# A recommendation network on one core: row transfers issued half by SyncE and half by ScalarE

## The chip, the cores and the metric

The kernel runs on one core of a Trainium2 chip. Its time is the device time of that core in microseconds (us), taken over several runs. Beside the times there is one profiled execution, whose trace holds every instruction of the five engines: PE (TensorE, matmuls; PEld are its weight loads), DVE (VectorE), ACT (ScalarE), POOL (GpSimd) and SP (SyncE). SP does no arithmetic; it only issues transfers. ACT and POOL issue transfers beside their own work. PEq, ACTq, SPq and so on are the sequencers, the parts of the engines that wait, load registers and issue transfers.

## The reference

The batch has 16384 samples. Each sample has 32 token numbers, three lists of 20 numbers, and four single numbers. All of them pick rows from tables:

```python
tok = word_emb[token_idx].mean(axis=1)      # 50000 x 300 table, 32 rows a sample
e1 = emb_mh1[mh1_idx].mean(axis=1)          # 1000 x 64, 20 rows a sample; e2: 5000 rows, e3: 10000
o1 = emb_oh1[oh1_idx]                       # 100 x 64; o2, o3, o4 alike
emb = jnp.concatenate([tok, e1, e2, e3, o1, o2, o3, o4], axis=1)     # 748 columns
wide = wide_mh1[mh1_idx].sum(...) + ... + wide_oh4[oh4_idx][:, 0]    # one number a sample
h = relu(emb @ W1 + b1)                     # 748 -> 1024
h = relu(h @ W2 + b2)                       # 1024 -> 512
h = relu(h @ W3 + b3)                       # 512 -> 256
return sigmoid(h @ Wd + bd + wide)          # 256 -> 1
```

All of it is float32. The token rows are the heavy part: 16384 x 32 rows of 1200 bytes.

## The kernel before, in words

The batch is cut into 128 tiles of 128 samples, one sample on each partition. Four kinds of work go on at once, and the kernel's main loop writes their instructions into one order by hand. The loop has 128 x 11 + 27 = 1435 steps, eleven for a tile and some at the end; what a step emits is the order in which each engine works it off.

**Small tables, by counting (PE, DVE, ACT).** The seven small tables stay in SBUF. In each step `one_hots` (line 501, DVE) compares index digits with a ramp and makes one-hot columns `hot`; ACT multiplies the upper half by 256 (line 508); `counts` (line 519, PE) multiplies pairs of one-hots into PSUM tiles `pc`; ACT copies them to `cnt` (line 522). There are two `hot` buffers and two `pc` buffers, and `hot` is made one step before PE uses it. `small_sums` (line 554, PE) multiplies the counts of the last tile with the tables, and DVE reduces the result into the feature tile `g` (line 544).

**The network (PE, ACT).** `g` is transposed by PE (line 595) and scaled by DVE into `x` (line 599); blocks of three tiles go through the three layers (line 677), and ACT applies bias and relu to each part of `h` (line 688). `ph` has two PSUM buffers.

**Token rows, by gather (POOL, DVE).** POOL issues an indirect transfer for each token place of a tile (line 337): it reads one row of the word table for each of the 128 samples into half of a buffer `tok_rows`. Six buffers hold two token places (a group) each. Three groups later (`TOK_LAG`) DVE adds the two halves to the tile's sum (lines 312, 314, 319). A buffer is free for the next gather when DVE has added it.

**Token rows, one by one (SP, ACT).** For some tiles a token place isn't gathered by POOL, and its 128 rows come as 128 single transfers of 1200 bytes whose addresses are registers (`fetch` on SP, `ScalarRows` on ACT):

- The column of 128 token numbers is loaded as one line (`load_column`), DVE turns it into byte offsets (lines 370, 371), and the queue's engine loads them into registers (line 375, TENSOR_LOAD: SP 32 at a time, ACT 8).
- SP fetches the last token place (31) of all tiles from 4 on whose number isn't a multiple of three: 83 tiles. `FETCH_AHEAD` says how many steps before the sum is due the fetch begins, `FETCH_STEPS` over how many steps its rows are spread in the order, `COLUMN_AHEAD` and `COLUMN_LAG` when column and offsets come.
- ACT fetches the last place but one (30) of tiles that `choose` picks: the first tile whose sum is due late enough for 128 rows at `SCALAR_RATE` rows a step and a margin of 5 steps. It does so for 26 tiles. Addresses are loaded at most twice a step, eight when fewer than eight are left (two when rows were issued just before).

What sets the order between these two is the lane. Every transfer of SP and ACT takes the next of eight semaphores (lanes) in a turn, and a lane's next transfer waits until its last one has landed. `transfers` holds the order over both queues. Lanes 6 and 7 of the turn belong to ACT: before SP takes one of them, `sync_dma` asks ScalarE for a row, and SP takes the lane itself only where ScalarE has no address ready:

```python
while len(transfers) % LANES in SCALAR_LANES and scalar_row and scalar_row[0]():
    pass
hardware_dma(nc.sync, **operands)
```

So in a turn of eight SP issues six and ACT two. ACT's rows stand in ACT's own order between the instructions on `hot`, `cnt` and `h`; an ACT row that waits holds up what stands behind it. The code line of all these transfers is line 161. SP also loads the indices of every pair of tiles, the weights at the start, and stores the outputs.

Of the kernel before, what the change touches and what calls it, by code (L numbers as in the profile page):

```python
# [26 lines left out]
TOK_BUFS = 6  # L27
HOT_BUFS = 2
FETCH_FROM = 4
FETCH_STEPS = 16.5  # L30
FETCH_AHEAD = {1: 25.0, 2: 19.5}
COLUMN_AHEAD = 4
COLUMN_LAG = 1
LOADS = 32
LANES = 8
SCALAR_LANES = (6, 7)
SCALAR_FROM = 12
SCALAR_RATE = 2.55
SCALAR_MARGIN = 5.0
SCALAR_LOADS = 8  # L40
SCALAR_WANTED, SCALAR_LEAST = 8, 2
# [43 lines left out]
def kernel(  # L85
# [85 lines left out]
    def sync_dma(**operands):  # L171

        while len(transfers) % LANES in SCALAR_LANES and scalar_row and scalar_row[0]():
            pass
# [222 lines left out]
    class ScalarRows:  # L397
# [9 lines left out]
        def choose(self, rows_before):  # L407

            least = self.step + (rows_before + P) / SCALAR_RATE + SCALAR_MARGIN
            t = next((t for t in range(tiles_all) if self.summed_at(t) >= least), None)  # L410
# [371 lines left out]
    tiles = B // P  # L782
# [13 lines left out]
    def summed_at(t):  # L796

        n = n_groups * (t + 1) + TOK_LAG
        return n / FRONT_PACE if n < front else FRONT_STEPS + (n - front) / pace

    fetches = [(summed_at(t) - FETCH_AHEAD[t % 3], t) for t in range(FETCH_FROM, tiles) if t % 3]
    fetching = []

    columns_due = []
# [1 line left out]
    def fetch_rows(step, part):  # L806
# [19 lines left out]
        for at, rows in list(fetching):  # L826
            rows.to(P * (step + part - at) / FETCH_STEPS)
            if step + part - at >= FETCH_STEPS:
                rows.finish()
# [9 lines left out]
    scalar = ScalarRows(summed_at, column_due)  # L839
    scalar_first = int(summed_at(SCALAR_FROM) - (P / SCALAR_RATE + 15))  # L840

# [29 lines left out]
    for step in range(n_steps):  # L871
        t, i = divmod(step, STEPS)
# [124 lines left out]
```

## Time and profile before

| | |
|---|---|
| time, median of 3 runs | 5021.99 us (5021.95 to 5024.2) |
| the profiled execution's own time | 5021.06 us |
| its span, first to last instruction | 5019.3 us |
| granted TensorE clock, mean | 0.990 |
| gathers on POOL (line 337) | 3987, 3773.3 us busy, 1219.3 us idle before them |
| rows issued by SP / by ACT | 10624 / 3328 |
| ACT busy / idle before its work | 2726.5 us / of which 1664.0 us waiting for DVE's `hot` |
| DMA engines, mean busy share; data | 0.48 in the steady part; 654 MB in all |

A line of a group of instructions names its code line, engine, operation, and what it writes and reads (out<-in), then how many there were, the shortest, median and longest duration in ns. "Idle before" is the time that the engine did nothing before such instructions, with what ended it. A wait line reads: who waited, for whom, us in total, how often, the longest. In a timeline each line is a start, a duration and an instruction; "x101" are so many alike that follow each other. The busy time of a sequencer (SPq, ACTq) isn't counted in the engine's busy share, so ACT's 54% holds none of its transfers.

### The profile page before, as it was taken

The numbers are of one execution on the slowest core, as the hardware profiler recorded it, in microseconds if no ns is written. First come the engines' busy times: TensorE is split into PE (matmuls) and PEld (weight loads), VectorE is DVE, ScalarE is ACT, GpSimd is POOL, SyncE is SP. The second block draws the span as 40 slices with busy tenths as digits, with TensorE's granted clock in tenths as the row PEclk, the third lists the DMA queues.
The fourth block names the chain that finished last, engine by engine and source line by source line (L and its number), as shares of the span: only waits on it lengthen the run. The fifth ranks groups of instructions, "written<-read, shape, count | busy, mean of one in ns | idle before, by whom it ended". The sixth has DMA issues, their size and how long they took to land.

```text
span 5019.3 us, 124363 instructions
## 1 busy us (share of the span) xinstructions
PE 4806.3 (96%) x36356; PEld 3721.3 (74%) x36356; DVE 3748.7 (75%) x6830; ACT 2726.5 (54%) x3658; POOL 3774.2 (75%) x3994
## 2 busy tenths in 40 slices
PE   6799999999999999999999999999999999999999
PEld 4577777777777777777777777667767888888899
DVE  6777777777777777777777777777777777777774
ACT  5455555555555555555555555555555555555552
POOL 7777777777777777777777777777777777777775
PEclk8899999999999999999999999999999999999999
DMA  7444444444444444444444444444444444444443
GB/s 204 127 129 130 129 129 129 129 130 129 129 130 128 129 130 129 130 129 129 129 129 129 130 129 129 130 129 129 130 130 129 129 129 130 130 129 130 129 128 100
DMA packets 291735, 654.13 MB, mean 130 GB/s; under 512 B 147100, under 2 KB 161692, under 8 KB 291048
## 3 DMA queue, kind: packets, MB, share of 16 engines
q0 software_dynamic: 191376, 612.66, 45.1%
q1 hardware_dynamic: 89271, 29.49, 2.7%
q10 hardware_dynamic: 10400, 4.02, 0.4%
q8 instruction: 284, 4.65, 0.4%
q14 instruction: 404, 3.30, 0.2%
HBM read 645.65 MB, written 0.07 MB: 129 GB/s over the span
## 4 chain that ended last, share of the span: by engine, by line
PE 37%; DMA 26%; DVE 15%; issue 12%; POOL 9%; ACT 1%; SPq 1%; ACTq 0%; DVEq 0%; POOLq 0%
DMA tok_rows<-in_word_emb_dram,it 23%; PE ph L677 17%; PE pg L554 14%; POOL tok_rows L337 9%; DVE hot L501 5%; DVE own L319 4%; PE pc L519 4%; DVE own L314 3%; DMA fetched_scalar<-in_word_emb_dram 1%; DMA fetched<-in_word_emb_dram 1%; PE pc L595 1%; DVE g L544 1%; PE po L719 1%; SPq L161 1%; DVE x L599 0%
## 5 line engine op out<-in xcount | busy, mean ns | idle before, releaser
L337 POOL DMA_INDIRECT tok_rows<-in_word_emb_dram,it x3987 | 3773.3, 946 | 1219.3 <-issue 754.1
L508 ACT ACTIVATE hot<-hot 64x768 bf16<-64x768 bf16 (+1 forms) x1408 | 1155.4, 821 | 1820.6 <-DVE hot L501 1664.0
L554 PE MATMUL pg<-terms,cnt 128*128 128x195 bf16 x17664 | 1723.7, 249 | 35.6 <-DVE g L544 35.0
L554 PEld LDWEIGHTS <-cnt 128*128 128x128 fp8e3 x17664 | 1529.2, 98 | 83.1 <-issue 54.4
L677 PE MATMUL ph<-x,w_sb 128*128 128x384 f32 (+5 forms) x4932 | 1473.8, 437 | 16.2 <-ACT h L688 11.9
L501 DVE TENSOR_TENSOR hot<-own,sc 128x1656 bf16<-128x1656 bf16 (+1 forms) x1408 | 1393.7, 990 | 126.7 <-PE pc L519 37.7
L522 ACT ACTIVATE cnt<-pc 128x828 uint16<-128x828 f32 (+1 forms) x1408 | 1186.5, 843 | 181.5 <-PE pc L519 103.2
L319 DVE TENSOR_TENSOR own<-own,tok_rows 128x300 f32<-128x300 f32 x1792 | 857.1, 478 | 513.3 <-DMA tok_rows<-in_word_emb_dram,it 468.5
L677 PE MATMUL ph<-h,w_sb 128*128 128x384 f32 (+2 forms) x4160 | 1225.9, 435 | 14.2 <-ACT h L688 14.0
L314 DVE TENSOR_TENSOR own<-own,tok_rows 128x300 f32<-128x300 f32 x1827 | 873.8, 478 | 271.9 <-DMA tok_rows<-in_word_emb_dram,it 221.0
L677 PEld LDWEIGHTS ph<-x,w_sb 128*128 128x128 f32 (+1 forms) x4932 | 830.8, 191 | 305.7 <-ACT h L688 23.0
L519 PEld LDWEIGHTS <-hot 128*128 128x128 bf16 x8192 | 594.2, 98 | 523.8 <-issue 271.3
L677 PEld LDWEIGHTS ph<-h,w_sb 128*128 128x128 f32 x4160 | 700.6, 191 | 266.1 <-ACT h L688 27.3
L519 PE MATMUL pc<-hot 128*128 128x138 bf16 x8192 | 733.1, 225 | 111.8 <-ACT hot L508 51.7
L688 ACT ACTIVATE h<-ph,b_sb 128x384 f32<-128x384 f32 (+2 forms) x723 | 378.7, 524 | 210.5 <-PE ph L677 115.4
L544 DVE TENSOR_REDUCE g<-pg 128x130 f32<-128x390 f32 (+1 forms) x512 | 259.2, 506 | 140.0 <-PE pg L554 138.7
L599 DVE TENSOR_TENSOR x<-pc,scale 128x768 f32<-128x768 f32 x127 | 120.8, 951 | 58.8 <-PE pc L595 57.5
L595 PE MATMUL pc<-ident,g 128*128 128x128 f32 x762 | 107.3, 278 | 5.7 <-ACT cnt L522 5.4
L312 DVE TENSOR_TENSOR own<-tok_rows 128x300 f32<-128x300 f32 x128 | 61.5, 481 | 55.3 <-DMA tok_rows<-in_word_emb_dram,it 52.6
L595 PEld LDWEIGHTS pc<-ident,g 128*128 128x128 f32 x762 | 83.7, 143 | 9.8 <-ACT cnt L522 9.3
L488 DVE COPY sc<-pc 128x512 bf16<-128x512 bf16 x64 | 44.0, 688 | 40.5 <-PE pc L484 39.8
L719 PE MATMUL po<-h,wd_sb 128*1 128x384 f32 (+2 forms) x208 | 67.4, 442 | 4.4 <-ACT h L688 4.4
(59 smaller groups left out, 514.6 us busy)
## 6 DMA issues: line engine op xcount, KB each, us to landing
fetched<-in_word_emb_dram SPq DMA_DIRECT2D x10624, 1.2 KB
tok_rows<-in_word_emb_dram,it POOLq DMA_INDIRECT x3987
fetched_scalar<-in_word_emb_dram ACTq DMA_DIRECT2D x3328, 1.2 KB
ix<-in_idx_dram SPq DMA_DIRECT2D x64, 64.0 KB
w_sb<-in_W_dram SPq DMA_DIRECT2D x6, 512.0 KB
raw<-in_mh_dram SPq DMA_DIRECT2D x4, 682.5 KB
it<-in_idx_dram SPq DMA_DIRECT2D x64, 32.0 KB
w_sb<-in_W_dram SPq DMA_DIRECT2D x1, 2048.0 KB
```

Source lines behind the costliest of these rows:

```text
L314: nc.vector.tensor_add(tok_sum, tok_sum, a)
L319: nc.vector.tensor_add(to, tok_sum, b)
L337: gather = nc.gpsimd.indirect_dma_start(out=rows[-1], out_offset=None, in_=word, in_offset=bass.IndirectOffsetOnAxis(ap=it[:, j : j + 1], ...
L501: nc.vector.tensor_tensor(hot[:, 0 : 2 * rows, :].rearrange("p i (n d) -> p i n d", d=2), iota.rearrange("p (n d) -> p n d", d=2).unsqueez ...
L508: nc.scalar.activation(upper, upper, AF.Copy, scale=UPPER)
L519: nc.tensor.matmul(pc[:, k // n, at : at + n_h], hot[:, 2 * k, 0:P], hot[:, 2 * k + 1, :], start=True, stop=True)
L522: nc.scalar.activation(cnt[:, :, b : b + rows].rearrange("l h (g k) -> l h g k", g=2), pc[:, :, 0 : n * n_h].rearrange("l g (k h) -> l h g ...
L544: nc.vector.tensor_reduce(field_columns(features(t), pair), pg[:, 0:n, :].rearrange("p f (c d) -> p f d c", c=3), AX.X, ALU.add,)
L554: nc.tensor.matmul(pg[:, j, :], by_slice[:, h, :], terms[:, h, :], start=(h == h0), stop=(h == h1 - 1))
L595: nc.tensor.transpose(pt[:, j // n, j % n, :], g[:, c : c + P], ident)
L677: nc.tensor.matmul(to, weights[: src.shape[0], k, m * P : (m + 1) * P], src, start=(k == 0), stop=(k == len(srcs) - 1),)
L688: nc.scalar.activation(dst()[:, m, 0:n], ph[:, 0:n], AF.Relu, bias=bias[:, m : m + 1])
```

## The change

The turn of lanes is dealt out anew: lanes 2, 3, 6 and 7 belong to ScalarE, so that a turn is two of SP, two of ACT, two of SP, two of ACT. SP fetches the last token place of every second tile (the odd ones from 5 on, 62 tiles for 83), each spread over 22 steps and begun 25.5 steps ahead. ACT's rate, by which `choose` picks the next tile, goes from 2.55 to 5.6 rows a step; ACT then fetches the last place but one of 53 tiles for 26. POOL's gathers go from 3987 to 3981. The order of all compute instructions on PE, DVE and ACT is the same in both kernels.

```diff
-FETCH_STEPS = 16.5
-FETCH_AHEAD = {1: 25.0, 2: 19.5}
+FETCH_STEPS = 22.0
+FETCH_EVERY = 2
+FETCH_AHEAD = {1: 25.5}
...
-SCALAR_LANES = (6, 7)
+SCALAR_LANES = (2, 3, 6, 7)
 SCALAR_FROM = 12
-SCALAR_RATE = 2.55
+SCALAR_RATE = 5.6
...
-    fetches = [(summed_at(t) - FETCH_AHEAD[t % 3], t) for t in range(FETCH_FROM, tiles) if t % 3]
+    fetches = [
+        (summed_at(t) - FETCH_AHEAD[t % FETCH_EVERY], t)
+        for t in range(FETCH_FROM, tiles)
+        if t % FETCH_EVERY in FETCH_AHEAD
+    ]
```

## The prediction

> **What bounds the kernel now.** I read the page's busy shares first. PE is at 96% and POOL at 75%, so PE looks like the bound; the second view, the instructions of the gather line L337, corrects that.
>
> ```profile
> PE 4806.3 (96%) x36356; PEld 3721.3 (74%) x36356; DVE 3748.7 (75%) x6830; ACT 2726.5 (54%) x3658; POOL 3774.2 (75%) x3994
> ```
> ```profile
> L337 POOL DMA_INDIRECT tok_rows<-in_word_emb_dram,it x3987: 942/946/1233, 2.8 to 4993.1; - x200
> ...
>   issue: 754.1, 2473
> ```
>
> A gather takes 946 ns, and the idle time before it is 754.1/2473 = 0.305 us, nearly always the same. Busy and idle time of the line are 3773.3 + 1219.3 = 4992.6 us over 3987 gathers, 1.252 us each, from 2.8 us to the end of the last at 4994.0. POOL therefore issues without a break for the whole run; only 18 of its starts lie over 1.3 us apart, and all that they lose is 5.4 us. After the last gather come 25.3 us of tail. POOL sets the time. But PE has little room, as the windows show (columns: busy us of PE, PEld, DVE, ACT, POOL, then clock and DMA share):
>
> ```profile
> 0.00:125.00 125.00, 84.16 (x496) 52.80 (x496) 78.35 (x157) 74.68 (x112) 93.49 (x105) 0.89 0.75 204
> 250.00:4900.00 4650.00, 4519.97 (x34082) 3487.59 (x34081) 3530.19 (x6404) 2560.97 (x3395) 3516.72 (x3717) 1.00 0.48 129
> ```
>
> Between 250 and 4900 us PE is idle for 130 us of 4650 (2.8%), at full clock. So there are two near-bounds, and whatever delays PE by more than that shows in the time. PE's waits in that stretch:
>
> ```profile
> PE pc L519 <- DVE x L599: 40.4, 39, 2.5
> PE pg L554 <- DVE g L544: 25.8, 30, 2.2
> PE ph L677 <- ACT h L688: 24.8, 29, 3.3
> PE pc L519 <- DVE sc L488: 11.9, 11, 2.0
> PE pc L519 <- ACT hot L508: 9.3, 14, 2.5
> ```
>
> Only waits of the counts (L519) on work that stands on DVE between gather-paced additions can shrink when gathers get fewer: 40.4 + 11.9 + 9.3 = 62 us. The rest are hand-overs.
>
> The third view is the two queues that issue single rows. Both also load addresses into registers (TENSOR_LOAD; 8 rows each on ACT, 32 on SP):
>
> ```profile
> L161 ACTq DMA_DIRECT2D fetched_scalar<-in_word_emb_dram x3328: 213/214/746, 309.9 to 4790.8; - x196
> L375 ACTq TENSOR_LOAD <-columns x416: 716/763/1013, 307.0 to 4770.6; - x139
> L375 SPq TENSOR_LOAD <-columns x332: 2025/2127/2373, 112.1 to 4953.7; - x166
> ```
> Their timelines and one wait (start, us taken, what):
> ```profile
> 2499.80 42.14 SPq L161 DMA_DIRECT2D fetched<-in_word_emb_dram  x101
> 2502.27 0.84 ACT L508 ACTIVATE hot<-hot 64x768 bf16<-64x768 bf16 x1 [3.19 <-DVE hot L501]
> 2502.35 0.53 ACTq L161 DMA_DIRECT2D fetched_scalar<-in_word_emb_dram  x2
> 2503.14 0.86 ACT L522 ACTIVATE cnt<-pc 128x828 uint16<-128x828 f32 x1
> 2504.16 0.59 ACTq L161 DMA_DIRECT2D fetched_scalar<-in_word_emb_dram  x2
> 2505.10 0.63 ACT L508 ACTIVATE hot<-hot 64x512 bf16<-64x512 bf16 x1 [1.10 <-DMA fetched_scalar<-in_word_emb_dram]
> ACT hot L508 <- DMA fetched_scalar<-in_word_emb_dram: 95.1, 92, 3.0
> ```
>
> ACT's rows are issued while an ACTIVATE runs (2502.35 inside 2502.27 to 2503.11), 0.32 us from start to start. A row on a lane waits until the lane's last transfer has landed: the second pair starts 1.81 us after the first, though cnt began at 2503.14, and it holds the next hot for 1.10 us. Over all rows the lane's semaphore moves a median of 1.94 us after the issue (1.6 to 2.2 from the tenth to the ninetieth percentile). Such lane waits cost ACT 95.1 us before hot, about 211 us in all.
>
> **The change part by part.** The program's order of compute is the same on every engine; only rows, loads and columns move.
>
> *Six gathers less.* SP fetches 62 tiles for 83, ACT 53 for 26: 115 rows of 128 for 109, so 3981 gathers for 3987. 6 x 1.252 = 7.5 us off POOL's path. Two address operations on DVE are added per tile, 12 in all of 0.22 us; DVE's idle share of 25% hides them.
>
> *ACT issues twice as much.* 6784 rows for 3328, 848 loads for 416, 53 columns for 26. Prices: 0.32 us a row; a load 0.763 us, and the row after it takes 0.45 us instead of 0.21, with the gap 1.07 us. I counted each ACTIVATE at the longer of its own duration and the issues that stand behind it in the order: 2.01 us a step before, 2.84 us after, of a step of 5019.3/1435 = 3.50 us. Often four rows (1.27 us) now stand under an ACTIVATE of 0.84 us. Queued behind them are hot (PE's counts wait for it), cnt and h. The cover is ACT's idle time, 2290 us in all, 1664 of it waiting for DVE's hot; and PE takes a hot a median of 1.8 us after ACT ends it, but within 0.3 us in 10% of the steps and within 1 us in 21%. Carrying the added 0.83 us from instruction to instruction through the idle times that the trace shows, hot is late for PE in 6% of the steps, 47 us in sum. Ends: 0 and 47 us; I take 47, since lateness was carried with the gaps as they stand.
>
> One rule bears on this. The Trainium skill, DMA: Bandwidth & Descriptors, section Issuing engines are not separate DMA queues, says that issuing from a further engine saves only the sequencer's time to issue, usually small beside the transfer. By it the move is worth nothing beyond the gathers, and the sum would be -7.5 us; the rows above show 0.32 us a row charged to a sequencer that also feeds PE.
>
> *SP has four lanes for six.* In the quoted stretch 101 rows take 42.1 us with three loads of 2.13 us in it: 0.354 us a row, 2.12 us for a turn of six lanes, so it is landing that paces SP. At four lanes that is 0.53 us a row. Two tiles (22 steps, 77.0 us) need 128 x 0.53 + 4 x 2.13 = 76.4 us, and some 2 us for index loads, the column and the store. About 6 of the 128 rows borrow ACT's lanes (next part), minus 3 us: 75.6 of 77.0, 98%. Before, 57.7 us held 128 x 0.354 + 8.5 + 1.5 = 55.3, 96%. This alone hides: it fits. Nor does a late SP reach DVE at once: the rows are asked for 25.5 steps ahead and issued over 22, so 3.5 steps (12 us) lie before the addition that reads them.
>
> The Trainium skill, Perfetto Trace Analysis, section DMA Instruction — HWDGE (DVE, Sync), says that the profiled window of such an instruction ends when the sequencer is free and does not hold the data movement. Reckoning with windows alone (214 ns and a move of 29 ns), SP would need 40 us of 77, and nothing would hold the 7.5 us back; the row-to-row times speak for 98%.
>
> *The queues get tied.* Lanes are handed out in program order. Where ScalarE has no address loaded at its turn, SP takes the lane; then SP's row waits for ACT's last row there to land, and ACT's next row there waits for SP's. In the order of the programs the owner of a lane changes 6 times before and 678 times after: about 340 times ACT waits for SP, and 338 times SP for ACT, once in four steps. In the trace ACT issues a median of 3.4 us after the SP row that precedes it in the program (-0.1 to 6.6 us from the fifth to the ninety-fifth percentile): SP runs ahead. Eight transfers are 8/11.1 of a step, 2.5 us, so at a crossing SP can keep a lead of only 2.5 - 1.94 = 0.6 us; the rest it waits. With 98% to do and a load of 2.13 us every 5.5 steps it then falls behind, and ACT, a compute engine, waits for SP's landing. Price of one such wait: between 0 and one landing, 1.94 us; no row shows it, and a gain is excluded, as a wait takes nothing away. The nearest row is ACT's own lane wait, 95.1/92 = 1.0 us when it occurs; as SP will be late at only part of the crossings I take 0.6 us. Spread over ACT and carried as above, PE's lateness grows from 47 to 101 us (187 at 1.0 us; at 1.94 us ACT no longer keeps up).
>
> **Sum.** Against the profiled execution's own time, 5021.1 us (1.8 around the span; the median of the runs is 0.9 above it). POOL's path: 5021.1 - 7.5 = 5013.6. PE's path: 5021.1 - 62 (waits that shrink) + 101 = 5060. The longer decides: 5060 us, 0.8% slower. PE becomes the bound, and POOL's gaps grow to about 45 + 5 us.
>
> **Rivals.**
> 1. Everything hides and POOL stays the bound: 5013.6 us. For it: ACT's 2290 idle us, the 1.8 us between hot and PE, three groups (7.5 us) of rows in front of POOL. Against it: PE's 130 us. It holds where a crossing costs ACT under about 0.2 us, for then PE's lateness is about 60 us and the 62 us that shrink pay for it. This is not slower.
> 2. SP becomes the bound: if each crossing holds SP for 1 us, two tiles need 75.6 + 5.8 = 81.4 us, 5.7% over 77.0; over the 4480 us in which ACT fetches, +250 us, 5270 us. For it: 98% full. Against it: a borrowed lane also gives back, and a longer step eases SP.
> 3. A gain beyond the gathers: POOL's 5.4 us of gaps vanish too: 5008 us. Nothing in the profile frees anything that feeds these gaps.
>
> That the change does not do what it says can be left out: the order of the changed program has the 3981 gathers.
>
> **Numbers.** About 0.2% (10 us) is what a measurement of this kernel can tell from no change; that puts "same" at 5012 to 5032. Chances: the forecast's mechanism 0.48, of which a tenth of the total ends below 5032 (a crossing near 0.4 us); rival 1 0.24, nearly all within 0.2% (0.20) and a little below (0.04); rival 2 0.24; rival 3 0.04. Faster 0.08, same 0.30, slower 0.62. The range leaves out the upper part of rival 2 and the gains: 5012 to 5230 us; the forecast's own is 5025 to 5146 (0.4 to 1.0 us a crossing).
>
> **What will show it.** Right: 3981 gathers, with idle time before them grown from 1219 us although they are fewer; ACT's waits on transfers grown from 211 us to 400 or more, some naming SP's rows (fetched); PE's counts waiting on ACT's hot for some 60 us instead of 9; SP's waits for ACT's rows appearing, its wait for columns on DVE (about 315 us now) gone. Wrong: gather after gather at 1.252 us with the end at 4986 us (rival 1), or SP without any wait but landings and PE's waits past 200 us (rival 2). The forecast fails first at the 0.6 us of a crossing, second at carrying lateness through idle times that would move with the rest.

## The result, and the profile after

The changed kernel takes 5049.6 us (median; 5040.9 to 5055.2) against 5022.0 us before: 1.0056 times as long, with a 95% interval of 1.0045 to 1.0067. The forecast was 5060 us, and it named POOL's growing gaps as the place where the time would show. That is where it shows. The cause that it put first is not borne out, as the runs below tell.

First the gather line and the stretch from 250 to 4900 us after the change (for gathers: shortest, median, longest duration in ns; then idle time before them; for the window: busy us of PE, PEld, DVE, ACT, POOL, clock, DMA share, GB/s):

```profile
L338 POOL DMA_INDIRECT tok_rows<-in_word_emb_dram,it x3981: 940/946/1207, 3.0 to 5021.6; - x200
...
  issue: 802.1, 2630
```
```profile
250.00:4900.00 4650.00, 4502.52 (x33801) 3459.76 (x33799) 3533.32 (x6386) 2540.68 (x3369) 3491.36 (x3690) 0.99 0.48 129
```

A gather takes 946 ns as before, and there are six fewer; but the last one ends at 5022.5 us for 4994.0, while the tail behind it is 25.3 us in both. So all of the loss is time in which POOL stands still. Taking every pair of starts more than 1.3 us apart, and what lies over 1.252 us in it, POOL loses 41.0 us where it lost 5.4. That settles the sum: 41.0 - 5.4 - 6 x 1.252 = 28.1 us, and 27.7 were measured.

The loss is not spread evenly. By stage (us lost by POOL; the small blocks of the network begin with tile 96, near 3760 us):

| stage | before | after |
|---|---|---|
| 0 to 3760 us | 2.1 | 3.6 |
| 3760 to 4750 us | 0.7 | 19.3 |
| 4750 us to the end | 2.6 | 18.1 |

For three quarters of the run the change costs POOL next to nothing. What makes POOL stop is that DVE adds rows late, because it waits for PE, and PE waits for ACT. First POOL's wait for the additions in the stage of the small blocks (3757 to 4700 us), before and after, and DVE's wait for PE between 250 and 4900 us, before and after:

```profile
POOL tok_rows L337 <- DVE own L319: 31.1, 102, 0.3
POOL tok_rows L338 <- DVE own L320: 33.9, 52, 2.6
DVE g L544 <- PE pg L554: 120.8, 106, 3.2
DVE g L545 <- PE pg L555: 318.7, 230, 7.6
```

A wait of 0.3 us is the usual gap between two gathers; now single waits reach 2.6 us. Then PE's waits after the change between 250 and 4900 us, and ACT's in the whole run, two of before and four of after:

```profile
PE ph L678 <- ACT h L689: 69.2, 66, 4.0
PE po L720 <- ACT h L689: 17.7, 19, 2.0
PE pc L596 <- ACT cnt L523: 17.1, 20, 2.7
PE pc L520 <- ACT hot L509: 13.7, 18, 2.5
PE pc L520 <- DVE x L600: 13.5, 12, 2.1
```
```profile
ACT h L688 <- DMA fetched_scalar<-in_word_emb_dram: 62.9, 84, 1.7
ACT cnt L522 <- DMA fetched_scalar<-in_word_emb_dram: 49.8, 67, 1.6
ACT hot L509 <- DVE hot L502: 717.0, 532, 5.1
ACT h L689 <- DMA fetched_scalar<-in_word_emb_dram: 306.9, 320, 2.8
ACT cnt L523 <- DMA fetched_scalar<-in_word_emb_dram: 306.4, 354, 2.3
ACT hot L509 <- DMA fetched_scalar<-in_word_emb_dram: 271.5, 271, 2.9
```

ACT's wait for DVE's hot, its reserve, falls from 1664 to 717 us, and its idle time before hot, cnt and h that ends with its own row transfers rises from 208 to 885 us. The sequencer's instructions in these stretches tell what filled them: rows being issued 79 us before and 320 now, address loads under 1 and 277, waits for a lane 83 and 186; the rest lies between its instructions. PE now waits longer for h (24.8 us before, 69.2 now) and for cnt (5.4, 17.1); for hot hardly longer (9.3, 13.7). A stretch of ACT's timeline shows how a row comes to hold up an ACTIVATE:

```profile
2503.28 0.84 ACT L509 ACTIVATE hot<-hot 64x768 bf16<-64x768 bf16 x1 [3.17 <-DVE hot L502]
2503.36 1.39 ACTq L162 DMA_DIRECT2D fetched_scalar<-in_word_emb_dram  x4
2504.79 0.86 ACT L523 ACTIVATE cnt<-pc 128x828 uint16<-128x828 f32 x1 [0.68 <-DMA fetched_scalar<-in_word_emb_dram]
2505.19 0.57 ACTq L162 DMA_DIRECT2D fetched_scalar<-in_word_emb_dram  x2
2506.21 0.63 ACT L509 ACTIVATE hot<-hot 64x512 bf16<-64x512 bf16 x1 [0.56 <-DVE hot L502]
2506.64 1.00 ACTq L162 DMA_DIRECT2D fetched_scalar<-in_word_emb_dram  x3
2508.58 0.58 ACT L689 ACTIVATE h<-ph,b_sb 128x384 f32<-128x384 f32 x1 [1.74 <-DMA fetched_scalar<-in_word_emb_dram]
```

Four rows take 1.39 us, but the hot above them runs for 0.84 us; cnt is held for 0.68 us. Later h is held for 1.74 us, behind three rows and a load of addresses, which these lines leave out (2507.68 to 2508.50).

SP's own waits, for the queue part, the first line before the change, the others after:

```profile
SPq L161 <- DMA fetched<-in_word_emb_dram: 132.3, 541, 0.6
SPq L162 <- DMA fetched<-in_word_emb_dram: 953.2, 2410, 1.4
SPq L162 <- DMA fetched_scalar<-in_word_emb_dram: 283.1, 195, 4.7
SPq L376 <- DVE own L315: 112.8, 21, 49.4
```

SP now waits for the landings of its own rows (132 us before, 953 now), and 195 times for one of ACT's.

### The profile page after: what moved, and what is told of

The parts are those of the page before. It is cut to its first block, busy times and chain, and to the rows that moved or that the text cites. A ratio compares the mean times of both kernels' runs of the same rounds, so it can differ in the third digit from the quotient of the medians.

```text
span 5047.8 us, 126270 instructions
## 1 busy us (share of the span) xinstructions
PE 4816.1 (95%) x36356; PEld 3719.7 (74%) x36356; DVE 3770.2 (75%) x6842; ACT 2723.3 (54%) x3658; POOL 3768.9 (75%) x3988
## 4 chain that ended last, share of the span: by engine, by line
PE 50%; DMA 22%; DVE 8%; issue 6%; ACTq 6%; POOL 3%; ACT 2%; SPq 1%; DVEq 0%; POOLq 0%
PE ph L678 24%; PE pg L555 19%; DMA tok_rows<-in_word_emb_dram,it 10%; DMA fetched_scalar<-in_word_emb_dram 9%; PE pc L520 5%; DVE hot L502 4%; ACTq L162 4%; POOL tok_rows L338 3%; DMA fetched<-in_word_emb_dram 3%; ACTq L376 2%; DVE own L320 2%; DVE own L315 1%; PE pc L596 1%; ACT h L689 1%; DMA columns<-in_idx_dram 1%
```

## The experiments

Each kernel is compared with the kernel before on the same chip. For the first four (up to the blocks of three) the kernel before took 5021 us, as in the prediction; this is called the first condition. For all that follow it took 7320 to 7420 us, the second condition: there the granted clock is 0.87, POOL waits over 2000 us for DVE, and PE, as far as the traces tell, sets the time. What those eight say holds for the second condition only.

### Addresses loaded earlier: the tie of the queues taken away

```diff
-SCALAR_WANTED, SCALAR_LEAST = 8, 2
+SCALAR_WANTED, SCALAR_LEAST = 8, 4
```

> The changed kernel, but ScalarE's addresses are loaded as soon as fewer than four are left (two before), so that it nearly always has one at its turn: the owner of a lane changes 18 times instead of 678. ACT fetches 58 tiles for 53 (928 loads for 848), POOL issues 3976 gathers. Theory A (the tie of the queues: ACT waits for SP's landing where a lane changes hands): POOL is gapless again, 11 gathers of 1.252 us fewer than the kernel before, 5022 - 14 = 5008 us (5004 to 5014), and ACT's waits on lanes fall far below the 885 us of the changed kernel. Theory B (ACT's own issue load: 0.32 us a row, 1.07 us a load): ACT issues 9% more than in the changed kernel, so 5050 us or above.

It took 5106.0 us, 1.017 times the kernel before (1.0156 to 1.0184). That is 56 us slower than the changed kernel, though a lane hardly ever changes hands. POOL lost 103 us, 39 of them before 3760 us. ACT's waits:

```profile
ACT hot L509 <- DVE hot L502: 510.7, 372, 4.6
ACT hot L509 <- DMA fetched_scalar<-in_word_emb_dram: 405.1, 357, 3.2
ACT cnt L523 <- DMA fetched_scalar<-in_word_emb_dram: 392.0, 360, 2.8
ACT h L689 <- DMA fetched_scalar<-in_word_emb_dram: 351.4, 325, 3.6
```

Theory A, the tie, falls as the cause: without it ACT waits more behind its rows (1148 us for 885). The run doesn't change the tie alone: SP no longer takes a share of ACT's turns, so ACT issues 9% more rows, and its loads come earlier, so that in these stretches they take 400 us for 277. The traces say the same of the single wait. Between 600 and 4700 us the changed kernel has 309 places where ACT's row follows a row of SP on its lane; ACT's sequencer waited over 0.15 us at 79 of them, 69 us in all, 0.22 us a place. It is SP that pays for the tie: 246 us at 181 of as many places, which its reserve covers. SP's lead over ACT in the program's order did shrink as foreseen, from a median of 3.4 us to 0.96 (0.6 was predicted), without harm to ACT.

### Loads alone, on the kernel before

```diff
-SCALAR_LOADS = 8
-SCALAR_WANTED, SCALAR_LEAST = 8, 2
+SCALAR_LOADS = 2
+SCALAR_WANTED, SCALAR_LEAST = 8, 8
```

> The kernel before with ACT's addresses loaded two at a time instead of eight: 1664 loads for 416, rows, lanes and gathers as they were (6 changes of a lane's owner). If a load of two takes about the 0.76 us of a load of eight, this adds 1248 x 0.76 = 950 us to ACT's sequencer, about 60% of the 1550 us that the change adds, without any new wait on a lane. Theory A (tie of the queues): 5022 us, within 5 us. Theory B (own issue load): 60% of the change's loss of 28 + 7.5 us, 5035 to 5050 us.

5022.1 us, 1.0003 times the kernel before (0.9994 to 1.0012). The loads did cost what was reckoned, and ACT's reserve fell to 1155 us:

```profile
L375 ACTq TENSOR_LOAD <-columns x1664: 489/780/1035, 307.2 to 4779.0; - x185
```
```profile
ACT hot L508 <- DVE hot L501: 1154.9, 830, 4.7
ACT cnt L522 <- DMA fetched_scalar<-in_word_emb_dram: 235.9, 250, 1.8
```

1248 more loads of 0.78 us are 973 us of issue, 63% of what the change adds, and POOL lost 6.1 us for 5.4. Theory B in its simple form, a price for each issue, falls too: up to here the issues hide altogether. They hid in part in time that ACT's sequencer had spent waiting for lanes: between 600 and 4700 us its waits of over 0.15 us fell from 558 to 97 us, so the run adds less to ACT than the loads alone. (By theory A the run had to come out as it did; the run before this one has already taken that theory out.)

### Blocks of three instead of two, in both kernels

```diff
-TWOS, ONES = 12, 8
+TWOS, ONES = 0, 8
```

> The changed kernel with the twelve blocks of two tiles replaced by blocks of three (tiles 96 to 119), which need less of PE a tile. In the changed kernel POOL's gaps begin at 3757 us, where these blocks begin. If the loss appears only where PE has no room left (theory P), POOL is gapless here up to the single-tile blocks, and this is 5 to 8 us faster than the kernel before with the same replacement. If lateness itself stops POOL wherever it is (theory A or B without P), it stays 20 us or more slower than that one.

> The kernel before with the same replacement, the reference for the changed kernel with it. POOL sets its time in either case: 5022 us, within 10 us (the work that follows the last gather is the same). PE's busy time falls.

With these blocks the changed kernel takes 5036.0 us and the kernel before 5040.0 us: now the change is 4 us faster. POOL lost 6.4 us (2.6 in the kernel before); the last gather ends at 4987.4 us, against 4991.1. Six gathers less are -7.5 us, the gaps +3.8, together -3.7. Both took longer than the kernel before only because the work behind the last gather grew from 25 to 46 us, which the second expectation had wrong. The stage from 3757 to 4700 us, in the kernel before with its blocks of two and then with blocks of three:

```profile
3757.00:4700.00 943.00, 923.46 (x7394) 801.70 (x7395) 722.50 (x1304) 529.43 (x729) 713.40 (x754) 1.00 0.49 129
```
```profile
3757.00:4700.00 943.00, 910.47 (x6689) 669.82 (x6687) 719.08 (x1305) 515.88 (x669) 713.09 (x755) 0.99 0.48 129
```

Blocks of three need 13 us less of PE and 60 ACTIVATEs less. So the loss of the changed kernel belongs to the stage of the small blocks, and goes when that stage is relieved. Behind 4750 us POOL's loss fell from 18.1 to 3.4 us as well, though the blocks of one tile at the end are the same in both: that part of the loss goes with the stage ahead of it. Whether PE's room or ACT's decides there, this run doesn't tell apart, as the blocks relieve both.

### Reading the first four together

With the two kernels they give one picture, which is a correlation over six kernels and no more. The share of a stage in which ACT waits for something of DVE is its reserve; beside it stands what POOL lost in the stage, in us (250 to 3757 us, then 3757 to 4700 and for POOL to 4750):

| kernel | reserve, first stage | POOL lost | reserve, small blocks | POOL lost |
|---|---|---|---|---|
| before, blocks of three | 38% | 2 | 38% | 0 |
| before | 1270/3507 = 36% | 2 | 298/943 = 32% | 1 |
| loads of two | 27% | 1 | 22% | 1 |
| changed, blocks of three | 22% | 2 | 22% | 1 |
| changed | 20% | 2 | 15% | 20 |
| changed, addresses early | 15% | 39 | 15% | 43 |

At 20% or more POOL loses nothing worth naming; at 15% it loses tens of us, in whichever stage that is. That fits a reserve that is used up in bursts, ahead of the mean: an ACTIVATE that comes 1 to 2 us late finds PE waiting, where PE is busy for 97 to 98% of the time. It is not shown: only three entries stand at 15%, and an engine that is late waits less for others, so the small share may follow from the loss.

### Rows one by one instead of in pairs

```diff
-SCALAR_LANES = (2, 3, 6, 7)
+SCALAR_LANES = (1, 3, 5, 7)
```

> The changed kernel with ScalarE's lanes 1, 3, 5, 7 for 2, 3, 6, 7: one of SyncE, one of ScalarE in turn. As many rows (6912 on ACT, 54 tiles, 3980 gathers) on as many lanes, and 602 changes of a lane's owner for 678; but between two ACT instructions there stand four or more rows at 130 places for 769, and three at 1656 for 281. Theory C (rows bunched in fours outlast the 0.84 us of the ACTIVATE over them and make ACT late): ACT waits more for DVE's hot again (717 us in the changed kernel) and POOL loses half or less of 41 us: 5014 to 5030 us. Theory L (the number of rows and their lanes' waits count, not how they are bunched): 5040 to 5056 us.

> The same kernel as the run with one of SyncE and one of ScalarE in turn, whose comparison fell on a chip that granted TensorE 0.88 of its clock and where POOL no longer sets the time. On a chip as that of the prediction the two theories expect what they did: theory C (rows bunched in fours outlast the ACTIVATE over them) 5014 to 5030 us, POOL losing half or less of 41 us; theory L (the number of rows and their lanes' waits count) 5040 to 5056 us.

Both comparisons fell on the second condition: 7369.2 us for 7338.4, ratio 1.0050 (1.0035 to 1.0065), and 7456.4 for 7415.5, 1.0050 (1.0036 to 1.0065). Whether bunching matters where POOL sets the time stays open. Here POOL lost about 2300 us in the first of these runs and 2430 in the second, and 2290 in the kernel before with six blocks of two (below); rows one by one cost 0.5% more than the kernel before.

### ACT stops fetching at tile 96

```diff
-            if t is None or t > tiles_all - 3:
+            if t is None or t > 96:
```

> The changed kernel, but ACT picks no tile above 96, so that in the stage of the small blocks (from 3757 us on) ACT issues nearly no rows and SP has all lanes. 3994 gathers. If ACT's rows in the stage where PE has no room make the loss (C or L with theory P), POOL is gapless throughout and sets the time: 5022 + 7 x 1.252 = 5031 us (5026 to 5036). If the loss comes of SP's part or of an earlier stage, POOL loses 20 us or more as well: 5050 to 5075 us.

7326.9 us for 7338.4, ratio 0.9988 (0.9974 to 1.0001): no difference that can be told, with seven gathers more. The expected times don't apply.

### Six blocks of two, in both kernels

```diff
-TWOS, ONES = 12, 8
+TWOS, ONES = 6, 8
```

> The changed kernel with six blocks of two tiles for twelve (tiles 108 to 119 instead of 96 to 119). By theory P POOL has no gaps up to tile 108 (4235 us), and loses only what it lost behind that, some 20 to 28 us of 41: 5025 to 5040 us, if the work behind the last gather doesn't grow. If lateness adds up over the run and only comes out late, 5045 to 5055 us.

> The kernel before with six blocks of two tiles for twelve: the reference for the changed kernel with them. POOL sets its time: 5022 us, up to 5030 if the work behind the last gather grows.

7365.5 us for the changed kernel with them, 7317.0 for the kernel before with them. In this condition, with these blocks, the change itself costs 48.5 us, 0.66%, more than where POOL sets the time (27.7 us). A likely reason, not tested, is that where PE is the bound throughout, ACT's lateness isn't covered in any stage. The kernel before gains 0.24% (0.9965 to 0.9988) from the larger blocks. For the stages in the first condition the two runs say nothing.

### The tie taken away at equal rows

```diff
-SCALAR_WANTED, SCALAR_LEAST = 8, 2
+SCALAR_WANTED, SCALAR_LEAST = 8, 4
...
-            least = self.step + (rows_before + P) / SCALAR_RATE + SCALAR_MARGIN
+            least = self.step + (rows_before + P) / SCALAR_RATE + SCALAR_MARGIN + (0 if rows_before else 8)
...
-            if t is None or t > tiles_all - 3:
+            if t is None or t > tiles_all - 3 or self.step % 150 < 24:
```

> As the run with addresses loaded below four, but ACT picks no tile in 24 of every 150 steps, so that it fetches 52 tiles, as good as the changed kernel's 53 (832 loads, 3982 gathers), with 100 changes of a lane's owner for 678. If the changes of owner make the loss (theory A), POOL loses few us: 5022 - 5 x 1.252 = 5016 us (5012 to 5025). If ACT's rows make it (theory C or L), about as slow as the changed kernel or slower, since the rows stand closer where ACT has any: 5045 to 5100 us.

7477.4 us for 7418.8, ratio 1.0071 (1.0046 to 1.0096). In this condition too a kernel with few changes of owner (100 for 678), and about as many rows as the changed one, is no better than its relatives (1.0050 with single rows). This supports what the first experiment showed, but it is no test in the condition of the prediction.

### Loads one at a time, on the kernel before

```diff
-SCALAR_LOADS = 8
-SCALAR_WANTED, SCALAR_LEAST = 8, 2
+SCALAR_LOADS = 1
+SCALAR_WANTED, SCALAR_LEAST = 8, 8
...
             scalar.load(scalar.issued == issued)
+            scalar.load(scalar.issued == issued)
```

> The kernel before with ACT's addresses loaded one at a time: 3328 loads for 416; rows, lanes, gathers as they were. With loads of two (780 ns each, 973 us more on ACT's sequencer) nothing was lost. Here some 2912 loads of 0.6 to 0.78 us are added, 1750 to 2270 us, more than the change adds. Theory F (whatever fills ACT makes it late, lanes or not): ACT waits for DVE's hot 700 us or less, and 30 to 80 us are lost, 5050 to 5100 us, in the stage of the small blocks first. Theory L (the added lane waits are what counts): 5022 to 5028 us.

7453.4 us for 7418.8, ratio 1.0047 (1.0032 to 1.0063). Rows, lanes and gathers are those of the kernel before; only ACT's sequencer has more to do (3328 loads, here of 0.45 us in the median). So issue alone can cost time where PE sets it. Whether it would in the first condition, at a reserve below 20%, wasn't seen.

### Half of each: the changed kernel, and the kernel before from tile 96 on

```diff
-FETCH_STEPS = 22.0
-FETCH_EVERY = 2
-FETCH_AHEAD = {1: 25.5}
+TURN_TILE = 94
+CHOOSE_EARLY = 36
+FETCH_STEPS = 22.0, 16.5
+FETCH_EVERY = 2, 3
+FETCH_AHEAD = {1: 25.5}, {1: 25.0, 2: 19.5}
...
-SCALAR_LANES = (2, 3, 6, 7)
+SCALAR_LANES = (2, 3, 6, 7), (6, 7)
...
-SCALAR_RATE = 5.6
+SCALAR_RATE = 5.6, 2.55
...
+    def late_turn(ahead=0):
+        return int(bool(scalar_row) and scalar_row[0].step + ahead >= scalar_row[0].summed_at(TURN_TILE + 3) - 25)
...
```

> The changed kernel up to about tile 96, the kernel before behind it: from the step at which the fetch for tile 97 begins, lanes 6 and 7 alone are ScalarE's, SP fetches for two tiles of three over 16.5 steps, and ACT's rate is 2.55 rows a step. 3983 gathers, 736 loads and 5888 rows on ACT. If the loss lies in the small blocks alone, where PE has no room (theory P), POOL is gapless throughout: 5022 - 4 x 1.252 = 5017 us (5013 to 5020), faster than both kernels. If ACT's rows in the long first stage leave something behind that comes out late, POOL loses 15 us or more: 5030 to 5050 us. On a chip that holds TensorE's clock down, where PE sets the time everywhere, ACT's rows cost there too: 0.2 to 0.5% more than the kernel before.

7356.6 us for 7322.2, ratio 1.0045 (1.0027 to 1.0062), as the last sentence of the expectation has it. Where POOL sets the time this is the version that the stages speak for, by some 5 us; it was not measured there, so no version is shown to beat the kernel before.

## Why the prediction was right or wrong

- **POOL as the bound, 1.252 us a gather, six gathers less:** right. The sum of gathers and gaps gives the measured time within 0.4 us.
- **The forecast time and its place:** 5060 us predicted, 5049.6 measured; POOL's gaps 50 us predicted, 41 measured. Rival 1 (everything hides, 5013.6 us) holds nearly up to 3760 us, and half of its gain shows with blocks of three (-4 us of -7.5). Its condition, a crossing under about 0.2 us, was all but met (0.22 us), and the loss came all the same. Rival 2 (SP becomes the bound) did not come about.
- **"The queues get tied", 0.6 us a crossing:** this step failed. The sequencer's wait was 0.22 us a crossing, and without crossings the kernel was slower. The term of 54 us (101 - 47) was much too large.
- **"ACT issues twice as much", 47 us:** too small, as far as the runs tell: without crossings (addresses loaded earlier, 9% more rows) PE's waits for ACT between 250 and 4900 us were 165 us, for 47 in the kernel before. What ACT stood idle behind its rows before hot, cnt and h grew by 677 us; 242 us of it are rows being issued, 277 address loads and 102 waits for a lane. The lane waits of the sequencer as a whole hardly grew (558 to 575 us of waits over 0.15 us between 600 and 4700 us); but two or four rows now fill the cover of an ACTIVATE, and what stood under it before stands beside it now. No run in the first condition separates rows, loads and lane waits.
- **The sum on PE's path:** luck in part. Between 250 and 4900 us all of PE's waits for ACT grew by 74 us (47 to 122), where 101 were forecast, and all its waits for DVE shrank by 57 (81 to 24), where the prediction had 62 (9 of them for hot, which is ACT's). So the term for the tie stood in for what the term for ACT's issues lacked.
- **"PE's counts waiting on ACT's hot for some 60 us":** wrong. That wait is 13.7 us; h and cnt are what PE waits for, some 104 us in the three lines quoted. I had carried lateness to hot alone, though h stands behind the same rows and `ph` has two buffers.
- **62 us of PE's waits that shrink:** half right; the three went from 61.6 to 31.0 us, and PE's wait for DVE's g, which had been taken for a hand-over that stays, from 25.8 to 4.2.
- **SP 98% full, its wait for columns gone:** mis-sized. SP's rows follow each other at 0.60 us, the pace of the program, and SP still waits for DVE at its loads: 235 us, for 314 before. Turns of four lanes are paced by landing (953 us of waits), but they fit. The pace of 0.354 us a row before was mostly issue and not landing, as the prediction read it: the median row followed the last at 0.32 us, and SP waited 132 us for landings over 10624 rows.
- **Lateness spread over the run:** not so. The stages differ, and the carrying should have been done stage by stage, where PE's idle share was 3.0% (250 to 3757 us) and 2.1% (to 4700).

## What to carry to other kernels

An engine that computes and issues transfers hides its issues under its own instructions only as far as they fit there one by one: count the issues and address loads behind each instruction, and carry the lateness to everything that stands behind them (here h and cnt, not hot alone). Look at the engine's reserve stage by stage; a change that is free in three quarters of the run can be paid for in the last. When a forecast names a new wait, size it from the sequencers' starts and ends, and test it by taking it away: here the total came near while the wait that was to explain it was nearly free.

## What the runs showed of the hardware that was not expected

A register load of two addresses on ACT takes as long as one of eight: 780 and 763 ns in the median. The Trainium skill, DMA: Bandwidth & Descriptors, section Latency and other measured facts, gives a floor of some 600 ns for a tensor_load; in the kernel before the loads of eight took 716 ns or more, while the shortest loads of two took 489 ns, under that floor, and loads of one, in the second condition, 454 ns in the median.

The same kernel can take 46% longer on a chip in another condition. From the page of the kernel before with six blocks of two, and PE's part of its timeline:

```profile
PE 5648.1 (77%) x35992; PEld 4052.2 (55%) x35992; DVE 3771.7 (51%) x6830; ACT 2731.4 (37%) x3628; POOL 3772.7 (51%) x3994
PEclk7788888888888888888888888888888888888888
```
```profile
2040.60 0.32 PE L554 MATMUL pg<-terms,cnt 128*128 128x195 bf16 x1 [1.16 <-issue]
...
2041.31 0.33 PE L554 MATMUL pg<-terms,cnt 128*128 128x195 bf16 x1 [0.39 <-issue]
2042.00 0.28 PEld L677 LDWEIGHTS ph<-h,w_sb 128*128 128x128 f32 x1 [0.60 <-issue]
2042.70 1.44 PE L677 MATMUL ph<-h,w_sb 128*128 128x384 f32 x2 [1.05 <-issue]
```

DVE, ACT and POOL are as busy in us as in the first condition. PE is busy for some 840 us more, and it stands still some 620 times for more than 1 us (1300 us in all; some 75 times and 140 us in the kernel before in the first condition). In the quoted stretch it starts its instructions 0.70 us apart and waits for nothing that the profile shows. The granted clock alternates between full and half there, half for a quarter of the time in the quoted run, 2% in the first condition. Whether the low clock causes the standstills or follows from them, and what holds PE, the runs don't tell.
